# A four-layer graph network on one core: the second linear layer on halves of the array's rows, and edge updates that gather target rows as three bf16 products

## The chip, the cores and the metric

The kernel runs on one core of a Trainium2 chip. The metric is the device time of one execution, in microseconds (us). The core has five engines with a queue each: PE (TensorE) with a side queue PEld for its weight loads, DVE (VectorE), ACT (ScalarE), POOL (GpSimd) and SP (SyncE, which here only issues DMAs). Each engine takes its own instructions in order.

## The reference, cut to what matters

12500 nodes of 16 features, 412500 directed edges (400000 and one loop per node) with 8 features each. Four graph layers run one after the other, each after a layer norm and a relu:

```python
h = relu(layernorm(x)); x = x + L0(h)   # tensor-product message, summed at row ends
h = relu(layernorm(x)); x = x + L1(h)   # message by an edge's own 16x16 matrix
h = relu(layernorm(x)); x = x + L2(h)   # encoder, then two rounds of the block below
h = relu(layernorm(x)); x = x + L3(h)   # two graph convolutions
```

Layer L2 is the one the change is about. With 64 features per node and edge:

```python
def _mlp(x, w0, b0, w1, b1):
    return silu(x @ w0 + b0) @ w1 + b1
n = _ln(_mlp(node_feat, ...)); e = _ln(_mlp(edge_feat, ...))     # encoder
for s in range(2):
    ce = concatenate([e, n[senders], n[receivers]], axis=-1)
    e = e + _ln(_mlp(ce, edge_blk_w0[s], edge_blk_b0[s], edge_blk_w1[s], edge_blk_b1[s]), ...)
    agg = segment_sum(e, receivers, num_segments=num_nodes)
    n = n + _ln(_mlp(concatenate([n, agg]), node_blk_w0[s], ...), ...)
```

So every edge has its feature vector multiplied by a first matrix, the sender's and receiver's rows added (they are multiplied per node beforehand), a silu, a second 64x64 matrix (the "second linear layer"), a layer norm, and a sum at its receiver.

## The kernel before, in words

**Nodes and slots.** Nodes are padded to 12544 and lie in 98 windows of 128 targets. A sort puts every edge into a slot of its target's window: per window 32 blocks of 128 regular slots, ordered by the sender's cell, and 5 blocks of overflow slots (TC, TO; TT is 37).

**Prologue.** Weights and biases are loaded to on-chip tiles by DMAs on SP's queue (`load_w`, `load_b`, `pair_diag`, `bias_rows`, L103 to L289), the sum arrays in DRAM are set to zero from a memory tile of zeros (L322 to L327), then X is loaded, normed (`relu_ln`, L1600) and multiplied to a first message table (`table128`, L1602).

**Sort.** `sort_edges` (L366 on) first finds where each window's edges start (`window_starts`, which loads all targets as `ws_di` and counts on DVE). Then a loop over 98 windows and 5 more steps (LAG) has an order written out by hand: `look_up`, `rank` on DVE, `scatter` on POOL (35 indirect DMAs of a window's records to `cells`, L597), and the layer-L0 products of the window five steps back.

**Pair stages.** The encoder (`Encoded`) and the edge updates 0 and 1 (`Updated`, `l2_cells(s)`) run over 49 pairs of windows in `over_pairs` (L1300). A pair has 10 chunks: c = 0 to 7 with 4 regular blocks, c = 8 with 4 overflow blocks, c = 9 with 1. The order of PE, DVE, ACT and SP is written by hand: slot c of the loop carries work of the new pair (first layer and silu of chunk c, second layer of chunk c−1) and of the old pair (normalizing and summing at targets). Per slot, in this order: `load_features` (SP), `hot_rows(c+1)`, `hidden(c)`, for the old pair `normed` (at c = 0), `scale(c)` and `features(c-1)`, then `output(c-1)`, `activate(c)`, `to_targets(c-1)`, and DVE's reduction. A pair starts with `start()` and `hot_rows(0)`; it ends with `total` (tile got2, on ACT).

**One chunk of an edge update on PE**, in the code's names:

- L1507: the edge features by w0e, on four 64x64 quadrants of the array, for two chunks at once.
- L1514, two forms, called by the helper `half`: first the target rows `td` (64 columns) by the one-hot tile `hot_dt`, 128x256 at a time (L1520), then the table of sender rows by the one-hot tile `hot_st` (32 small products, "hs" below). Two column halves of the array are used in turn.
- L1254: transposes of the old pair's y (edge update 0 and encoder).
- L1216 and L1218 (`outs`): bias as a product of ones, then for each block one product with a 128x128 block-diagonal weight: two slots' 64 features share the 128 rows.
- L1273 (`to_targets`): sums at targets by one-hot rows hot2, 16 instructions.

**The other engines in a chunk.** DVE makes `hot_dt` and `hot_st` (L1490, L1491, L1494 for overflow: is_equal of byte places and the partition's number), reduces squares (L1224), scales y (L1233) and makes hot2 (L1238). ACT does silu (L1209), squares and copies the second layer's result out of PSUM (L1221, L1223), and lod, got2 once a pair. POOL fetches overflow senders' rows (L1467, indirect DMAs).

**PSUM.** The 8 banks in these stages are pt=2, po=5, pa=1; hidden and outs take from po.

**Node tables.** Before an edge update, `tables_l2` (L1648) multiplies the nodes to a table of 128 columns; `take` puts half of it in `t_src` and half, with the bias, in `t_dst` (f32). An update loads `td` from `t_dst`; for s = 1, DVE adds a row `be_w0e` to it at the start of each pair (L1479).

An older form in this kernel makes one-hot rows on ACT: a byte minus a column number, absolute (L630, L1059), then relu(1 − x) (L631, L1060).

Of the kernel before, what the change touches and what calls it, by code (L numbers as in the profile page):

```python
# [19 lines left out]
P = 128  # L20
# [27 lines left out]
def tile_gnn(ctx: ExitStack, tc: tile.TileContext, a: dict, out: bass.AP):  # L48
# [23 lines left out]
    usual = dict(pt=2, po=5, pa=1)  # L72
    summing = dict(pt=2, po=4, pa=2)

    def bank(tag):
        pool, bufs = now[0]
        return pool.tile([P, 512], F32, name=tag, bufs=bufs[tag])
# [53 lines left out]
    def pair_diag(name, src, centered):  # L131

        d = consts.tile([P, P], F32, name=name)
        two = consts.tile([P, 64], F32, name=name + "_2")
        v.memset(d, 0.0)
        sp.dma_start(two[0:64, :], src)
        sp.dma_start(two[64:128, :], src)
        if centered:
            center(two, 64)
        v.tensor_copy(d[0:64, 0:64], two[0:64, :])  # L140
        v.tensor_copy(d[64:128, 64:128], two[64:128, :])
        return d

    def bias_rows(name, src, centered):

        b = consts.tile([3, 64], F32, name=name + "_f")
        sp.dma_start(b, row_bc(src, 64, 3))
        if centered:
            center(b, 64)
        part = consts.tile([3, 3, 64], BF16, name=name + "_p")  # L150
# [10 lines left out]
        r = consts.tile([P, 8, 64], BF16, name=name)  # L161
        v.memset(r, 0.0)
        v.tensor_copy(r[0:3], acc[:, None, :].to_broadcast([3, 8, 64]))
        return r.rearrange("p t f -> p (t f)")
# [27 lines left out]
    wml = load_w("wml", a["L0_gnn_W_msg_lin"], 16, 16)  # L192
    v.tensor_scalar(wml, wml, 0.25, None, op0=ALU.mult)
    wupd = load_w("wupd", a["L0_gnn_W_upd_tp"].rearrange("i h k -> i (h k)"), 16, 256)
    v.tensor_scalar(wupd, wupd, 1.0 / 16.0, None, op0=ALU.mult)
    wul = load_w("wul", a["L0_gnn_W_upd_lin"], 16, 16)
    v.tensor_scalar(wul, wul, 0.25, None, op0=ALU.mult)
    w1t = load_w("w1t", a["L1_w_iao"], 16, 128)
    w1c = consts.tile([P, 16], F32, name="w1c")
    for j in range(8):  # L200
        sp.dma_start(w1c[16 * j:16 * j + 16, :], a["L1_w_iao"][:, 16 * j:16 * j + 16])
    b1_l1 = load_b("b1_l1", a["L1_gnn_bias"], 16)

    p2 = "L2_gnn_"
    ne_w0 = load_w("ne_w0", a[p2 + "node_enc_w0"], 16, 64)
    ne_b0 = load_b("ne_b0", a[p2 + "node_enc_b0"], 64)
    ne_w1 = load_w("ne_w1", a[p2 + "node_enc_w1"], 64, 64)
    center(ne_w1, 64)
    ne_b1 = load_b("ne_b1", a[p2 + "node_enc_b1"], 64)
    center(ne_b1, 64)  # L210
    ne_g = load_b("ne_g", a[p2 + "node_enc_g"], 64)
    ne_be = load_b("ne_be", a[p2 + "node_enc_beta"], 64)

    ee_w0 = consts.tile([P, 8, 64], F32, name="ee_w0")
    v.memset(ee_w0, 0.0)
    for t in range(TS):
        sp.dma_start(ee_w0[8 * t:8 * t + 8, t % 8, :], a[p2 + "edge_enc_w0"])
    ee_w0 = ee_w0.rearrange("p t f -> p (t f)")

    ec_w0 = consts.tile([P, 8, 64], F32, name="ec_w0")  # L220
    v.memset(ec_w0, 0.0)
    for t in range(8):
        sp.dma_start(ec_w0[WORDS * t:WORDS * t + 8, t, :], a[p2 + "edge_enc_w0"])
        sp.dma_start(ec_w0[WORDS * t + W_ONE:WORDS * t + W_ONE + 1, t, :], row_bc(a[p2 + "edge_enc_b0"], 64, 1))
    ec_w0 = ec_w0.rearrange("p t f -> p (t f)")
    ee_b0 = bias_rows("ee_b0", a[p2 + "edge_enc_b0"], False)
    ee_w1 = pair_diag("ee_w1", a[p2 + "edge_enc_w1"], True)
    ee_b1 = bias_rows("ee_b1", a[p2 + "edge_enc_b1"], True)
    ee_g = load_b("ee_g", a[p2 + "edge_enc_g"], 64)
    ee_be = load_b("ee_be", a[p2 + "edge_enc_beta"], 64)  # L230
# [8 lines left out]
    ee_g2 = twice("ee_g2", a[p2 + "edge_enc_g"])  # L239
    ee_be2 = twice("ee_be2", a[p2 + "edge_enc_beta"])  # L240

    eb, nb = [], []
    for s in range(2):
        w0, f = a[p2 + "edge_blk_w0"][s], {}
        f["w0e"] = pair_diag(f"eb_w0e{s}", w0[0:64, :], False)
        f["w0sd"] = consts.tile([64, 128], F32, name=f"eb_w0sd{s}")
        sp.dma_start(f["w0sd"][:, 0:64], w0[64:128, :])
        sp.dma_start(f["w0sd"][:, 64:128], w0[128:192, :])
        f["b0"] = load_b(f"eb_b0{s}", a[p2 + "edge_blk_b0"][s], 64)
        f["w1"] = pair_diag(f"eb_w1{s}", a[p2 + "edge_blk_w1"][s], True)  # L250
        f["w1x"] = consts.tile([P, P], F32, name=f"eb_w1x{s}")
        v.memset(f["w1x"], 0.0)
        sp.dma_start(f["w1x"][0:64, 64:128], f["w1"][64:128, 64:128])
        sp.dma_start(f["w1x"][64:128, 0:64], f["w1"][0:64, 0:64])
        f["b1"] = bias_rows(f"eb_b1{s}", a[p2 + "edge_blk_b1"][s], True)
        f["g"] = load_b(f"eb_g{s}", a[p2 + "edge_blk_g"][s], 64)
        f["be"] = load_b(f"eb_be{s}", a[p2 + "edge_blk_beta"][s], 64)
        f["g2"] = twice(f"eb_g2{s}", a[p2 + "edge_blk_g"][s])
        eb.append(f)
        f = {}  # L260
        f["w0"] = load_w(f"nb_w0{s}", a[p2 + "node_blk_w0"][s], 128, 64)
        f["b0"] = load_b(f"nb_b0{s}", a[p2 + "node_blk_b0"][s], 64)
        f["w1"] = load_w(f"nb_w1{s}", a[p2 + "node_blk_w1"][s], 64, 64)
        center(f["w1"], 64)
        f["b1"] = load_b(f"nb_b1{s}", a[p2 + "node_blk_b1"][s], 64)
        center(f["b1"], 64)
        f["g"] = load_b(f"nb_g{s}", a[p2 + "node_blk_g"][s], 64)
        f["be"] = load_b(f"nb_be{s}", a[p2 + "node_blk_beta"][s], 64)
        nb.append(f)

    eb[0]["sum_be"], eb[1]["sum_be"] = consts.tile([P, 64], F32, name="sum_be"), eb[1]["be"]
    v.tensor_add(eb[0]["sum_be"], eb[0]["be"], ee_be)

    be0 = twice("eb_be2", a[p2 + "edge_blk_beta"][0])
    be_w0e = consts.tile([P, 64], F32, name="be_w0e")
    with banks(**usual):
        pb0 = bank("pa")
        pe.matmul(pb0[:, 0:64], lhsT=be0[0:64, :].to_broadcast([64, P]), rhs=eb[1]["w0e"][0:64, 0:64], start=True,
                  stop=True)
        v.tensor_copy(be_w0e, pb0[:, 0:64])  # L280
    dec_w0 = load_w("dec_w0", a[p2 + "dec_w0"], 64, 64)
    dec_b0 = load_b("dec_b0", a[p2 + "dec_b0"], 64)
    dec_w1 = load_w("dec_w1", a[p2 + "dec_w1"], 64, 16)
    dec_b1 = load_b("dec_b1", a[p2 + "dec_b1"], 16)
    gw1 = load_w("gw1", a["L3_w1_t"], 16, 32)
    gb1 = load_b("gb1", a["L3_gnn_b1"], 32)
    gw2 = load_w("gw2", a["L3_w2_t"], 32, 16)
    gb2 = load_b("gb2", a["L3_gnn_b2"], 16)
# [34 lines left out]
    with tc.tile_pool(name="prep", bufs=1) as wk:  # L323
        zero = wk.tile([P, (C + 1) * 64], F32, name="zero")
        v.memset(zero, 0.0)
        for t in [*g_l0, g_l1, *g_l2, *g_gc, t_acc]:
            sp.dma_start(t.rearrange("(p c) d -> p (c d)", p=P), zero[:, :t.shape[0] // P * t.shape[1]])  # L327
# [1477 lines left out]
```

## Time and profile before

| | |
|---|---|
| Median of 11 runs | 19122.32 us (19106.53 to 19156.79) |
| The profiled execution's own time | 19120.87 us |
| Its span | 19119.1 us |
| PE, PEld, DVE, ACT, POOL busy | 12907.0, 10331.6, 12477.1, 6089.7, 7062.4 us |
| Mean granted TensorE clock | 0.791 |

| Stage | Span, us | Length | Share |
|---|---|---|---|
| Prologue | 0 to 178 | 178 | 0.9% |
| Sort and L0 products | 178 to 7240 | 7062 | 36.9% |
| Encoder and L0's rest | 7240 to 9380 | 2140 | 11.2% |
| L1 with its node work | 9380 to 10813 | 1433 | 7.5% |
| Node work, tables for update 0 | 10813 to 10986 | 173 | 0.9% |
| Edge update 0 | 10986 to 13922 | 2936 | 15.4% |
| Node work, tables for update 1 | 13922 to 14137 | 215 | 1.1% |
| Edge update 1 | 14137 to 16550 | 2413 | 12.6% |
| Rest: node work and L3 | 16550 to 19119 | 2569 | 13.4% |

How to read it. Stage bounds were read from the trace by where a stage's lines begin and end. The middle period of a pair, from one pair's lod copy (L1200) to the next, is 43.0 us in the encoder, 59.8 in edge update 0 and 48.8 in edge update 1. A group line has the line in the code, engine, operation, tile names (out<-in), shape, count, then busy time in us and mean ns of one, then the engine's idle time just before them and what ended it. PE instructions overlap, so the mean duration of one is longer than the time from one start to the next; for PE it is the start-to-start time that adds up. The granted clock is TensorE's, as a share of full speed.

### The profile page before, as it was taken

How to read it: one execution, taken by the hardware profiler on the slowest of the kernel's cores; microseconds unless marked ns; L12 is line 12 of the kernel's file. 1: busy time of each engine (PE TensorE's matmuls, PEld its weight loads, DVE VectorE, ACT ScalarE, POOL GpSimd, SP SyncE). 2: the span in 40 equal slices, each digit the busy share in tenths (PEclk: the TensorE clock that was granted, in tenths of full speed). 3: DMA queues.
4: the chain of work that ended last, by engine and by line, in shares of the span. 5: the costliest groups of instructions: out<-in, count | busy, mean ns of one | idle time of the engine just before them, and what ended most of it. 6: DMA issues, size and time to landing. Idle time of an engine off the chain costs nothing. (4 is left out here: it accounts for less than half of the span.)

```text
span 19119.1 us, 387064 instructions
## 1 busy us (share of the span) xinstructions
PE 12907.0 (68%) x161327; PEld 10331.6 (54%) x161327; DVE 12477.1 (65%) x23622; ACT 6089.7 (32%) x10025; POOL 7062.4 (37%) x6387
## 2 busy tenths in 40 slices
PE   1444444444444448999788688888879999756566
PEld 1443434444443447777577666666656666644444
DVE  5555555555555556777788777777757777655555
ACT  0111111111111125555377522222223333334343
POOL 3444444444444443444344311111113322144344
PEclk6666666666666669999899899999989999966666
DMA  1101100001000004444366544444434333266666
GB/s 67 28 25 28 28 28 25 28 28 28 25 28 28 25 24 105 126 125 126 107 169 172 145 130 136 136 136 135 135 109 118 116 114 115 75 172 176 160 175 169
DMA packets 1361577, 1827.92 MB, mean 96 GB/s; under 512 B 501594, under 2 KB 794970, under 8 KB 1358526
## 3 DMA queue, kind: packets, MB, share of 16 engines
q1 hardware_dynamic: 1079624, 1721.34, 29.6%
q0 software_dynamic: 258720, 76.68, 4.1%
q8 instruction: 1275, 20.89, 0.5%
q10 hardware_dynamic: 21462, 4.95, 0.1%
q14 instruction: 496, 4.06, 0.1%
HBM read 1296.64 MB, written 504.92 MB: 94 GB/s over the span
## 5 line engine op out<-in xcount | busy, mean ns | idle before, releaser
L597 POOL DMA_INDIRECT cells<-rec,s_row x3430 | 3295.5, 961 | 3632.0 <-DVE s_row L593 2527.5
L1467 POOL DMA_INDIRECT xo<-t_src,c x980 | 1246.3, 1272 | 4424.2 <-DMA c<-cells 2207.2
L641 PE MATMUL pl<-win,hot_dt 128*128 128x128 f32 x7252 | 1445.8, 372 | 2110.9 <-DVE wide L650 1736.5
L641 PEld LDWEIGHTS pl<-win,hot_dt 128*128 128x128 f32 x7252 | 1342.5, 281 | 2177.1 <-DVE wide L650 1774.0
L650 DVE TENSOR_TENSOR wide<-pl,c 128x512 f32<-128x512 f32 x980 | 602.9, 645 | 2726.2 <-remote 2519.8
L675 PE MATMUL acc<-parted,hot_s 128*98 128x64 f32 x6272 | 1186.1, 344 | 1676.6 <-issue 1663.9
L675 PEld LDWEIGHTS acc<-parted,hot_s 128*98 128x98 f32 x6272 | 1101.4, 266 | 1781.8 <-issue 1765.3
L1221 ACT ACTIVATE sq<-po 128x512 f32<-128x512 f32 (+1 forms) x1470 | 832.3, 566 | 3694.1 <-PE po L1218 2853.3
L1273 PE MATMUL pa<-hot,y 128*64 128x128 f32 x21756 | 1674.8, 284 | 240.2 <-issue 155.0
L1224 DVE TENSOR_REDUCE nsum<-sq 128x8 f32<-128x512 f32 (+1 forms) x1470 | 947.1, 644 | 1141.7 <-ACT sq L1221 1099.9
L1011 POOL DMA_INDIRECT xo<-t_gc,c x980 | 1032.4, 1054 | 1586.2 <-DMA c<-cells 556.8
L1238 DVE TENSOR_TENSOR hot<-iota_row,lod 128x512 f32<-128x512 f32 x2352 | 1517.3, 687 | 0.0
L1273 PEld LDWEIGHTS pa<-hot,y 128*64 128x64 f32 x21756 | 1211.9, 138 | 529.1 <-issue 334.8
L812 POOL DMA_INDIRECT g_l<-summed,row x490 | 857.7, 1750 | 1411.9 <-ACT summed L808 1075.9
L1082 DVE TENSOR_REDUCE x<-po 128x128 f32<-128x384 f32 x1176 | 650.9, 553 | 1048.1 <-remote 470.4
L666 ACT ACTIVATE parted<-pre 32x256 f32<-32x256 f32 x784 | 325.1, 415 | 3157.8 <-issue 2913.3
L1514 PE MATMUL po<-hot_dt,td 128*64 128x256 f32 (+2 forms) x7056 | 1012.7, 404 | 9.9 <-DVE hot_dt L1490 8.5
L631 ACT ACTIVATE hot_dt<-off,one_col 128x2048 f32<-128x2048 bf16 (+1 forms) x294 | 473.9, 1612 | 1652.6 <-remote 1631.1
L1059 ACT ACTIVATE off<-places,minus_col 98x1024 bf16<-98x1024 uint8 x784 | 898.9, 1147 | 269.5 <-DMA places<-slot_lo 224.5
L1209 ACT ACTIVATE hidn<-po 128x512 f32<-128x512 f32 (+1 forms) x1470 | 855.9, 582 | 329.1 <-PE po L1514 269.4
L1233 DVE TENSOR_TENSOR y<-y,nr 128x512 f32<-128x512 f32 (+1 forms) x1470 | 949.2, 646 | 5.1
L1091 DVE TENSOR_TENSOR hot_d<-iota_row,c 128x1024 f32<-128x1024 f32 (+1 forms) x882 | 949.6, 1077 | 0.0
(380 smaller groups left out, 27677.7 us busy)
## 6 DMA issues: line engine op xcount, KB each, us to landing
hot_dk<-keep_t SPq DMA_DIRECT2D x588, 512.0 KB
e_feat<-ft SPq DMA_DIRECT2D x882, 256.0 KB
ft<-e_feat SPq DMA_DIRECT2D x882, 256.0 KB
c<-cells SPq DMA_DIRECT2D x392, 296.0 KB
keep_t<-hot SPq DMA_DIRECT2D x392, 256.0 KB
ud<-slot_lo SPq DMA_DIRECT2D x98, 1024.0 KB
c<-cells SPq DMA_DIRECT2D x147, 592.0 KB
us<-slot_lo SPq DMA_DIRECT2D x98, 784.0 KB
```

The costliest lines, as they stand in the source:

```text
L597: ins = gp.indirect_dma_start(out=self.cells, out_offset=bass.IndirectOffsetOnAxis(ap=self.row[:, t:t + 1], axis=0), in_=self.rec[:, t, :] ...
L641: pe.matmul(pl[:, t * P:(t + 1) * P], lhsT=self.hots[t0 // 16][:, o:o + P], rhs=self.win, start=True, stop=True, skip_group_check=True)
L675: pe.matmul(acc[t // 8][0:C, o:o + 64], lhsT=self.hot[:, t, :], rhs=self.k["parted"][self.g % 2][:, t, :, :].rearrange("p q f -> p (q f)") ...
L1011: gp.indirect_dma_start(out=out[:, t, :], out_offset=None, in_=table, in_offset=bass.IndirectOffsetOnAxis(ap=c[:, TC + t, W_SRC:W_SRC + 1] ...
L1059: sc.activation(off, u, AF.Abs, bias=minus_col[:C, :])
L1091: v.tensor_tensor(o[:, :k, :], bc_mid(iota_row, k), bc_last(self.c[:, t0:t0 + k, W_LD], P), ALU.is_equal)
L1224: return lambda: v.tensor_reduce(self.sums[:, 8 * c:8 * c + 2 * k], sq[:, :2 * k, :], AX.X, ALU.add)
L1233: v.tensor_tensor(w, w, bc_last(self.r[:, 8 * c:8 * c + 2 * k], 64), ALU.mult)
L1238: v.tensor_tensor(hot[:, w].rearrange("p (h t) d -> p h t d", h=2), iota_row[:, None, None, :].to_broadcast([P, 2, 2, P]), lo[:, :, :, Non ...
L1273: pe.matmul(self.acc[64 * w:64 * w + 64, 0:P], lhsT=lhsT, rhs=rhs, start=c == 0 and i < 2, stop=c == 9 and i >= len(work) - 2, skip_group_ ...
L1467: gp.indirect_dma_start(out=self.xo[:, w, t, :], out_offset=None, in_=t_src[s], in_offset=bass.IndirectOffsetOnAxis(ap=self.c[:, w, TC + t ...
L1514: pe.matmul(out[o:o + 64], lhsT=lhsT, rhs=rhs, start=start, stop=stop, skip_group_check=True)
```

## The change

Four edits come together.

1. **Second layer.** `outs` works on row halves: for each block two products, rows 0 to 63 and rows 64 to 127 of the array, each with a 64x64 weight, into the two banks of a new tile `pw` (one buffer of two banks; po goes from 5 to 3). The bias is two products of up to 256 columns. ACT's square and copy read both banks by one access pattern. The tile y goes from 12 to 11 buffers.
2. **Target rows.** `td` is loaded from a new DRAM table `t_dst3` of three bf16 parts, whose sum is exactly the f32 row; `hot_dt` is bf16, and each product becomes three.
3. **One-hot rows by ACT.** `hot_dt` is made by ACT (Abs, then Relu, with a one-buffer tile `off`) in place of DVE, and `hot_rows` runs two chunks ahead in place of one (3 buffers); `activate(c)` comes before `output(c-1)`.
4. **Prologue.** The weights' loads, their centering and the zeroing of DRAM sums become steps of a generator `weights`, one of which is taken at the start of each step of the sort's loop; `window_starts` runs first, and X is loaded after the targets.

`tables_l2` writes the three parts: ACT copies to bf16, POOL subtracts; for s = 1 it adds `be_w0e` there.

```diff
-    usual = dict(pt=2, po=5, pa=1)
+    usual = dict(pt=2, po=3, pa=1, pw=1)
...
+    def weights(zero):
...
+        for name, src, centered in pairs:
+            d = consts.tile([P, P], F32, name=name)
+            two = consts.tile([P, 64], F32, name=name + "_2")
+            v.memset(d, 0.0)
+            sp.dma_start(two[0:64, :], src)
+            sp.dma_start(two[64:128, :], src)
+            diags[name] = (d, two, centered)
+            yield
...
+        n = zero.shape[1]
+        for t in [*g_l0, g_l1, *g_l2, *g_gc, t_acc]:
+            w = t.shape[0] // P * t.shape[1]
+            for o in range(0, w, n):
+                k = min(n, w - o)
+                sp.dma_start(t.rearrange("(p c) d -> p (c d)", p=P)[:, o:o + k], zero[:, :k])
+                yield
...
+                zero = one.tile([P, C * 17], F32, name="zero")
+                v.memset(zero, 0.0)
+                others = weights(zero)
                 for g in range(ND + LAG):
+                    if g:
+                        next(others, None)
...
-            k, po, hid = self.blocks(c), bank("po"), self.hid
-            n = k * P
-            pe.matmul(po[:, :n], lhsT=ones_r, rhs=b1[:, :n], start=True, stop=False, skip_group_check=True)
+            k, pw, hid = self.blocks(c), bank("pw"), self.hid[c]
+            for half in range(2):
+                pe.matmul(pw[:, half, :k * 64], lhsT=ones_r, rhs=b1[:, :k * 64], start=True, stop=False,
+                          skip_group_check=True)
             for j in range(k):
-                pe.matmul(po[:, j * P:(j + 1) * P], lhsT=hid[:, j * P:(j + 1) * P], rhs=w1, start=False,
-                          stop=j == k - 1, skip_group_check=True)
+                for h in range(2):
+                    x, half = slice(64 * h, 64 * h + 64), h ^ swapped
+                    pe.matmul(pw[:, half, j * 64:(j + 1) * 64], lhsT=hid[x, j * P:(j + 1) * P],
+                              rhs=w1[x, 64 * half:64 * half + 64], start=False, stop=j == k - 1, skip_group_check=True)
+            out = pw[:, :, :k * 64].rearrange("p h (j f) -> p j h f", f=64)
             sq = self.ed.tile([P, 8, 64], F32, name="sq")
-            sc.activation(flat(sq)[:, :n], po[:, :n], AF.Square)
-            self.ys[c] = self.ed.tile([P, 4, P], F32, name="y", bufs=12)
-            sc.copy(flat(self.ys[c])[:, :n], po[:, :n])
+            sc.activation(sq[:, :2 * k, :].rearrange("p (j h) f -> p j h f", h=2), out, AF.Square)
+            self.ys[c] = self.ed.tile([P, 4, P], F32, name="y", bufs=11)
+            sc.copy(self.ys[c][:, :k, :].rearrange("p j (h f) -> p j h f", h=2), out)
...
                     new.hot_rows(0)
+                    new.hot_rows(1)
...
-                    if new and c < 9:
-                        new.hot_rows(c + 1)
+                    if new and c < 8:
+                        new.hot_rows(c + 2)
...
+                    if new and c < 10:
+                        new.activate(c)
                     if new and c:
                         reduce = new.output(c - 1)
-                    if new and c < 10:
-                        new.activate(c)
...
-                    v.tensor_scalar(hd, of(self.ud), iota_col, None, op0=ALU.is_equal)
+                    u, o, d = of(self.ud), off, hd
                     v.tensor_scalar(hs, of(self.us), iota_col[:C, :], None, op0=ALU.is_equal)
...
+                sc.activation(o, u, AF.Abs, bias=minus_col)
+                sc.activation(d, o, AF.Relu, bias=one_col, scale=-1.0)
...
-                        for h in range(2):
-                            half(h, po[:, 2 * w * P:2 * (w + 1) * P], self.td[:, w, :], hd[:, w, h, :])
+                        for part in parts:
+                            for h in range(2):
+                                half(h, po[:, 2 * w * P:2 * (w + 1) * P], self.td[:, w, part], hd[:, w, h, :])
...
+    with tc.tile_pool(name="ws", bufs=1) as wk:
+        window_starts(wk)
...
+            for j in range(3):
+                sc.copy(parts[:, :k, j, :], was[:, :k, :])
+                if j < 2:
+                    gp.tensor_tensor(rest[:, :k, :], was[:, :k, :], parts[:, :k, j, :], ALU.subtract)
+                was = rest
+            sp.dma_start(rows(t_dst3[s])[:, c:c + k, :], parts[:, :k].rearrange("p k j f -> p k (j f)"))
```

## The prediction

> **What bounds the kernel now.** I read the sums by stage first, because the engine shares of the whole run mix eight stages. Columns: length, busy time of PE, PEld, DVE, ACT and POOL with instruction counts, granted TensorE clock, DMA share, GB/s.
>
> ```profile
> 0.00:178.00 178.00, 27.83 (x69) 12.97 (x70) 92.93 (x209) 3.19 (x5) 5.64 (x16) 0.88 0.36 134
> 178.00:7240.00 7062.00, 3072.96 (x17248) 2825.20 (x17247) 4005.48 (x6863) 1317.70 (x1585) 3295.64 (x3431) 0.62 0.10 27
> 7240.00:9380.00 2140.00, 1996.60 (x19306) 1558.60 (x19306) 1580.25 (x3479) 1212.41 (x2303) 856.93 (x490) 0.99 0.46 124
> 10986.00:13922.00 2936.00, 2626.47 (x32237) 1928.14 (x32235) 2176.49 (x4109) 756.50 (x1566) 539.52 (x484) 0.93 0.47 134
> 14137.00:16550.00 2413.00, 2265.37 (x30424) 1667.18 (x30421) 1876.65 (x3670) 756.50 (x1567) 692.89 (x484) 0.99 0.39 113
> ```
>
> Row by row: prologue, sort, encoder, edge update 0, edge update 1. The last three are PE's (93, 89 and 94% busy); the sort is not (44%). In the sort one wait rules, by the page:
>
> ```profile
> L597 POOL DMA_INDIRECT cells<-rec,s_row x3430 | 3295.5, 961 | 3632.0 <-DVE s_row L593 2527.5
> ```
>
> POOL waits 2527.5 us for DVE's ranks, about 26 us in each of 98 windows: there DVE work adds directly.
>
> Then one chunk of edge update 0, as the timeline shows it (start, time covered):
>
> ```profile
> 12003.85 0.38 PE L1216 MATMUL po<-eb_b,ones_r 128*128 128x512 bf16 x1
> 12003.85 1.08 PEld L1218 LDWEIGHTS po<-eb_w1x,hidn 128*128 128x128 f32 x8
> 12004.07 1.05 PE L1218 MATMUL po<-eb_w1x,hidn 128*128 128x128 f32 x8
> 12005.05 0.85 PEld L1273 LDWEIGHTS pa<-hot,y 128*64 128x64 f32 x16
> ...
> 12010.59 0.21 PEld L1507 LDWEIGHTS po<-ft,eb_w0e 64*64 64x64 f32 x8 [0.17 <-issue]
> ```
>
> From L1218's start to that of L1273's first load is 0.98 us: eight instructions (an f32 matmul is two) at 112 ns, plus 0.09 for the change of tile shape. Is 112 ns the moving side's price or the weight load's? Another line loads the same 128 f32 columns and moves only 16:
>
> ```profile
> L806 PEld LDWEIGHTS po<-over,same x980: 186/192/192, 7295.1 to 9370.9; 128*128 128x128 f32 x196
> L806 PE MATMUL po<-over,same x980: 262/263/283, 7295.1 to 9370.9; 128*128 128x16 f32 x196
> ```
>
> Its starts are also 112 ns apart and its durations nearly L1218's (280 and 193 ns), so the load sets the pace. Last, the groups of edge update 1 that the change touches or that show its start-of-pair wait:
>
> ```profile
> L1273 PE MATMUL pa<-hot,y 128*64 128x128 f32 x7252 | 561.7, 281 | 102.9 <-DVE hot L1238 73.1 <-issue 22.6 <-DVE hot L1243 0.2
> L1514 PE MATMUL po<-hot_dt,td 128*64 128x256 f32 (+1 forms) x3528 | 491.1, 395 | 8.2 <-DVE hot_dt L1490 8.2
> L1490 DVE TENSOR_SCALAR hot_dt<-ud,iota_col 128x1024 f32<-128x1024 uint8 x390 | 293.3, 752 | 2.6 <-PE po L1514 2.6
> L1209 ACT ACTIVATE hidn<-po 128x512 f32<-128x512 f32 x490 | 285.3, 582 | 139.7 <-PE po L1514 139.7
> L1218 PE MATMUL po<-eb_w,hidn 128*128 128x128 f32 x1960 | 275.2, 280 | 2.2 <-ACT hidn L1209 0.8 <-issue 0.2
> ```
>
> PE's largest wait is 73.1 us, 1.5 per pair of windows: to_targets(0) waits for DVE's first hot2, queued behind rsqrt. In edge update 0 that wait is about 2.07 per pair, seen as one run of L1514's 32 taking 3.1 us instead of 1.03 before the transposes at 12053.
>
> **The change part by part.** The sum is made against the profiled execution: span 19119.1, own time 19120.9 (1.8 around the span), 1.4 under the median 19122.3.
>
> *Second layer on halves (1470 chunks: 3 stages x 49 pairs x 10).* Eight instructions of 128 rows, 128 moving columns become sixteen of 64 rows, 64 moving columns, on two row halves. Each still loads 128 columns. L1507's eight loads (132 ns each, four quadrants, both row halves) lie in 0.21 us, so loads of different tiles run together; eight pairs at 112 ns are then what eight instructions are now. Added: one more change of shape, since the bias stays at full height (0.09 as at L1218 to L1273), an exposed first load (0.107, a 128-column load) less a shorter last product (0.054, the 64 columns): **+0.149 us per chunk**. Bounds: below, −0.28, if loads hide and the 58 ns per pair of L1514's hs rows (64 columns loaded and moved) holds: 8 x (58 − 112) + 149. Above, +1.05, if the halves' loads queue: 8 x 112 more. I take the value by L1507, the only row with both row halves loading at once.
>
> A rule speaks here. The Trainium skill, TensorEngine Tiling (Array Packing), Theoretical Speedup, gives up to 2x for a contraction of 64; by it the eight pairs would halve and the sum fall by some 630 us, as in rival one. The same page under Key Properties says changing the tiling mode drains the array, which speaks against the change, and this trace's 0.09 is that cost. TensorE: Matmul & The Clock Gate, LDWEIGHTS, says load time follows the columns and not the rows, as the 16-column row above suggests; by it the sum stays mine.
>
> *td as three bf16 parts.* Four pairs of 256 moving f32 columns at 215 ns become six. The bf16 price is not in this trace at this shape; a bf16 pass is one of the two f32 passes, so 109 ns (the cadence of L1273's 128 f32 columns, the same number of passes of columns). 864 − 654 = **−0.21 per chunk**, −1.95 per pair with the short last chunk; bounds −0.46 (58 per pair) and +0.43 (215 still). Beside it 13 more PE instructions per chunk; where PE waits for "issue" that may cost, and I put it at nothing because issue is 0.5% of edge update 1.
>
> *hot_dt by ACT.* DVE loses 0.75 us per chunk, ACT gains Abs and Relu: 1.15 each (L1059 and L1060, 98x1024, 1147 and 1150 ns). ACT's chunk goes from 1.7 to 4.0 us against PE's 4.5 to 5.1: it fits in steady running. Not at the start of a pair, where ACT's queue holds got (0.37), lod (0.31), Abs(0), Relu(0), Abs(1), Relu(1), Abs(2), Relu(2), then silu(0). PE ends the old pair's to_targets(9), does L1507 (1.02) and needs Relu(0): 0.1 + 0.37 + 0.31 + 2.3 + 0.1 − 1.02 = 2.2 idle, against 0.25 now, +1.95. Then silu(0) stands behind four more one-hot operations (4.6), and outs(0) behind it: PE has td(0), hs, td(1), hs, about 3.4, and waits some +0.57 after handoffs. The DVE wait at to_targets(0) (2.07, 1.5) goes: DVE's queue has 0.85 less ahead of rsqrt and PE arrives 2 later. Per pair, with td −1.95 and outs +1.49: edge update 0, −0.46 + 1.95 + 0.57 − 2.07 = 0.0; edge update 1, −0.46 + 1.95 + 0.57 − 1.5 = +0.56, taken +0.1 and +0.6. Encoder: outs alone, 1.49 x 0.93 busy = +1.4. 49 x 2.1 = **+103**. Bounds: one-hot operations at 1.0 give +20; at 1.3 +190; at 2.0 (L630's 2048 columns, twice the size) ACT's chunk would be 5.7, over PE's, about +700.
>
> *Clock.* The granted clock comes in windows of about 3.4 us: every window with PE under 0.4 busy is followed by half clock, about half of those between 0.45 and 0.6. Edge update 1 stays at 0.99 with worst windows at 0.56. A 2.2 us wait in one window leaves 0.35; alignment puts it there in about half of 98 pairs, and a half-clock window costs some 2.4: **+115** (0 to +330). The Trainium skill's clock gate section in TensorE: Matmul & The Clock Gate likewise ties idle windows to a half clock; the rows above are enough without it.
>
> *Node tables.* Each take (49 in all) adds three ACT copies of 128x256 (0.38 each, between L704's 0.27 at 128 columns and 0.587 at 512), two POOL subtractions and a DMA, in one chain with hand-offs: 2.5 us against the 1.22 that DVE takes now. 49 x 1.3 = **+65** (+20 if POOL and ACT overlap across takes; +110 if POOL needs 0.5 each). The DVE add leaving the pair start is 0.28 of cover only.
>
> *Prologue into the sort loop.* The weights' DMAs hold SP's queue to 56 us, the zeroing to 92; X lands at 92.7, and dst only at 143.7. With both gone, dst lands about 10, then window starts 29, layer norm 15, table 28, sort constants 6: 88 of 178, −90. Into the loop go 77 steps: about 100 small DVE instructions (0.14 as L128's, to 0.25 with gaps) and memsets, 27 us, on DVE's ranks that POOL waits for; the zeroing DMAs run where DMA is 10% busy. A late matmul +1. **−62** (−95 if DVE's steps fall beside POOL's transfers; 0 if each zeroing transfer also delays a window by 3.6).
>
> Sum: 19120.9 − 62 + 65 + 103 + 115 = 19343, about **19345**, +1.2%.
>
> **Rivals.** *One, faster: the row halves aren't bound by loads.* Then outs costs −0.28, not +0.149, per chunk: 19345 − 0.43 x 1470 = 18715. For it: loads of other tiles overlap matmuls in L1507. Against it: L806's rows. It decides wherever outs' cadence falls under 97 ns per pair, where the whole sum reaches 19120. *Two: the halves' loads queue.* 8 x 112 ns x 1470 = +1317, to 20660. For it: all loads come from one PE queue; against it: L1507. *Three: ACT's chain at the pair start is short or hidden, and tables overlap.* No clock loss (−115), pairs +20 (−83), tables +20 (−45): 19100, about what it is now; for it, ACT is 26 to 31% busy; against it, its in-order queue. *Four, within the first: the clock falls at every pair,* +215 more, 19560.
>
> **How the numbers follow.** 0.2%, 38 us, is about what a measurement of this kernel can tell from no change. Forecast (19180 to 19620, its own range) 0.57; rival one 0.20; rival two 0.11; rival three 0.12, of which 0.05 is faster, 0.06 the same and 0.01 slower. So faster 0.25, same 0.06, slower 0.69. The range runs from rival one's time to just over the forecast's own, 18715 to 19700; rival two and the tails stay outside.
>
> **What would show it.** Right: outs' pairs 112 ns apart with about 1.13 us from its first start to to_targets'; td's group 0.65; PE at a pair's start waiting about 2 us for ACT's hot_dt; ACT near 75% busy in both updates; clock under 0.95 in edge update 1; prologue about 90, sort about 27 longer. Wrong: outs' pairs near 58 or 224 ns; a one-hot operation far from 1.15; the wait at the start taken by nobody. The sum fails most easily at the cadence of the row halves, which no row shows, and next at the clock.

## The result and the profile after

The changed kernel takes 19561.5 us (median of 8 runs, 19522.7 to 19623.5) against 19126.0 (31 runs): ratio 1.023, interval 1.022 to 1.024, 436 us slower. The forecast had the sign and half the size (+223), inside its range. The profiled execution of the changed kernel has a span of 19573.6 us, 454.5 more than before.

The sums by stage of the changed kernel, in the same columns and order as before (prologue, sort, encoder, edge update 0, edge update 1):

```profile
0.00:82.00 82.00, 25.08 (x63) 11.63 (x63) 63.05 (x90) 3.30 (x5) 3.55 (x14) 0.99 0.29 109
82.00:7138.00 7056.00, 3045.74 (x17254) 2803.78 (x17254) 4032.40 (x6982) 1317.77 (x1586) 3297.47 (x3434) 0.62 0.10 29
7138.00:9306.00 2168.00, 2032.36 (x23422) 1575.12 (x23422) 1579.98 (x3478) 1207.59 (x2303) 867.99 (x487) 1.00 0.46 122
10948.00:14043.00 3095.00, 2694.94 (x38121) 2086.45 (x38121) 1898.74 (x3622) 1791.24 (x2547) 475.43 (x490) 0.89 0.45 128
14274.00:17000.00 2726.00, 2403.06 (x36309) 1870.84 (x36309) 1575.46 (x3133) 1794.10 (x2548) 563.00 (x490) 0.91 0.35 102
```

Both updates grew, update 1 by twelve per cent, and their granted clock fell to 0.89 and 0.91. The 454.5 us by stage, each cut at the first lod copy and the last got2 of its pairs:

| Stretch | Before | After | Difference |
|---|---|---|---|
| Prologue and sort, to the encoder's first pair | 7244.7 | 7137.9 | −107 |
| Encoder | 2131.6 | 2167.6 | +36 |
| L1, node work, tables for update 0 | 1601.0 | 1642.7 | +42 (tables 27) |
| Edge update 0 | 2945.3 | 3095.1 | +150 |
| Node work, tables for update 1 | 204.2 | 230.9 | +27 |
| Edge update 1 | 2421.5 | 2725.2 | +304 |
| Rest | 2570.8 | 2574.2 | +3 |

Where in a pair? One steady chunk of the changed kernel in the timeline:

```profile
15407.74 0.85 PE L1558 MATMUL po<-hot_dt,td 128*64 128x256 bf16 x12
...
15408.42 1.10 PE L1558 MATMUL po<-hot_st,tab 98*64 98x64 f32 x32
...
15409.45 0.39 PE L1255 MATMUL pw<-eb_b,ones_r 128*128 128x256 bf16 x2
...
15409.77 1.11 PE L1260 MATMUL pw<-eb_w1x,hidn 64*128 64x64 f32 x16
```

td's twelve take 0.68 before the hs products start (0.86 to 0.91 before), the bias 0.32 (0.23 before) and the sixteen row-half products 1.04 up to to_targets at 15410.81 (0.98 before). A steady chunk is 0.06 us shorter: not the loss. The waits of PE in update 1, in total, number of times and longest; first of the changed kernel, then of the kernel before:

```profile
PE po L1558 <- ACT hot_dt L1539: 112.8, 87, 1.9
PE po L1558 <- issue: 106.6, 208, 1.1
...
PE pw L1260 <- issue: 30.9, 58, 1.0
...
PE pw L1255 <- issue: 16.6, 26, 1.1
PE pa L1316 <- DVE hot L1281: 6.1, 8, 4.9
```

```profile
PE pa L1273 <- DVE hot L1238: 73.1, 56, 4.9
...
PE pa L1273 <- issue: 22.6, 90, 1.0
...
PE po L1514 <- issue: 5.9, 9, 1.2
```

At the start of a pair a wait for ACT's hot_dt took the place of the one for DVE's hot2, as forecast. New is "issue": PE waits for nothing that the profile shows, in the middle of a group whose data has long been there. Part of one such place:

```profile
15418.33 0.96 POOL L1511 DMA_INDIRECT xo<-t_src,c  x1 [0.30 <-issue]
15418.46 1.03 PEld L1558 LDWEIGHTS po<-hot_st,tab 98*64 98x64 f32 x25
15418.57 1.07 PE L1558 MATMUL po<-hot_st,tab 98*64 98x64 f32 x24
15419.60 0.94 POOL L1511 DMA_INDIRECT xo<-t_src,c  x1 [0.30 <-issue]
15419.99 0.36 PE L1558 MATMUL po<-hot_st,tab 98*64 98x64 f32 x5 [0.36 <-issue]
...
15420.72 0.22 PE L1558 MATMUL po<-hot_st,tab 98*64 98x64 f32 x1 [0.38 <-issue]
15420.85 0.95 POOL L1511 DMA_INDIRECT xo<-t_src,c  x1 [0.31 <-issue]
15421.43 0.19 PEld L1558 LDWEIGHTS po<-hot_st,tab 98*64 98x64 f32 x2 [1.18 <-issue]
15421.44 0.33 PE L1558 MATMUL po<-hot_st,tab 98*64 98x64 f32 x2 [0.50 <-issue]
```

One group of 32 starts at 29 per us for 0.8 us, and then its last eight come a few at a time, 0.7 us apart, while POOL issues one indirect load of xo (rows of overflow senders) after another. I call this the slow stretch. Adding up each group of a pair over its undisturbed length (means over the pairs whose groups come in the same order, us a pair): between the second w0e group and the overflow chunks, update 0 lost 9.0 before and 11.9 after, update 1 lost 2.6 and 8.35. (In plain times from the second w0e group to the first overflow product: 41.46 and 43.68 us in update 0, where the undisturbed runs e6 and e5 below have 32.51 and 31.84; 32.22 and 37.23 in update 1, against 29.63 and 28.95.) So (2.9 + 5.7) x 49 = 420 us of growth in the slow stretch; starts of pairs +1.14 and +1.40, 124 us; the remainder of the two stages is shorter by some 90. All the rest of the program nets to about nothing.

### The profile page after: what moved, and what is told of

Same layout as the page of the kernel before. It is cut to its first block, busy times and chain, and to the rows that moved or that the text cites. A ratio compares the mean times of both kernels' runs of the same rounds, so it can differ in the third digit from the quotient of the medians.

```text
span 19573.6 us, 419284 instructions
## 1 busy us (share of the span) xinstructions
PE 13138.0 (67%) x177203; PEld 10699.4 (55%) x177203; DVE 11904.1 (61%) x22618; ACT 8211.6 (42%) x12135; POOL 6944.0 (35%) x6487
## 5 line engine op out<-in xcount | busy, mean ns | idle before, releaser
L1511 POOL DMA_INDIRECT xo<-t_src,c x980 | 1038.4, 1060 | 4645.7 <-DMA c<-cells 2345.1
L1264 ACT ACTIVATE sq<-pw 128x512 f32<-128x512 f32 (+1 forms) x1470 | 831.1, 565 | 1017.1 <-PE pw L1260 752.0
L1558 PE MATMUL po<-hot_st,tab 98*64 98x64 f32 x25088 | 1042.8, 234 | 149.9 <-issue 145.2
L1558 PE MATMUL po<-hot_dt,td 128*64 128x256 bf16 (+2 forms) x10584 | 886.9, 297 | 307.5 <-ACT hot_dt L1539 229.0
L1558 PEld LDWEIGHTS po<-hot_st,tab 98*64 98x64 f32 x25088 | 979.4, 149 | 193.1 <-issue 188.6
L1539 ACT ACTIVATE hot_dt<-off,one_col 128x1024 bf16<-128x1024 bf16 x980 | 1065.0, 1087 | 31.9
```

Source lines behind the costliest of these rows:

```text
L1264: sc.activation(sq[:, :2 * k, :].rearrange("p (j h) f -> p j h f", h=2), out, AF.Square)
L1511: gp.indirect_dma_start(out=self.xo[:, w, t, :], out_offset=None, in_=t_src[s], in_offset=bass.IndirectOffsetOnAxis(ap=self.c[:, w, TC + t ...
L1539: sc.activation(d, o, AF.Relu, bias=one_col, scale=-1.0)
L1558: pe.matmul(out[o:o + 64], lhsT=lhsT, rhs=rhs, start=start, stop=stop, skip_group_check=True)
```

## The experiments

The first runs were to tell two theories of the stretch apart. S: the bulk transfers for the next pair fill the DMA engines and PE's instructions are late, the more so as PE has more of them (13 more per chunk). R: one-hot rows two chunks ahead free the byte-place tiles us and ud a slot sooner, so these transfers fall on denser chunks.

**Row halves alone (e1)**, on the kernel before: the new `outs` and `pw` only.

```diff
-    usual = dict(pt=2, po=5, pa=1)
+    usual = dict(pt=2, po=3, pa=1, pw=1)
```

> The kernel before with the second layer on row halves alone (nothing else of the change). Both theories: steady chunks 0.15 us longer, +222 over 1470 chunks, since the pairs of row-half products still start 112 ns apart. Theory S (PE runs short of instructions while the next pair's transfers fill the DMA engines, the more so the more instructions a chunk has): the slow stretch near chunk 6 or 7 also grows in both edge updates, 9 of the change's 13 added PE instructions per chunk being here; of its growth of 377 us some 260, so about 19600. Theory R (the stretch grew because one-hot rows two chunks ahead free the byte-place tiles a slot earlier, so the transfers fall on denser chunks): the stretch stays as before, about 19345.

Measured 19402.0 against 19117.9, ratio 1.0137 (1.0115 to 1.0159), +284. The steady price is as both theories had it; the stretch lost 8.9 and 3.7 us a pair against 9.0 and 2.6, +51. Nine more PE instructions per chunk do not make 377.

**bf16 target rows alone (e2)**, on the kernel before:

```diff
-                self.td = td = ed.tile([P, 2, 64], F32, name="td")
...
+                self.td = td = ed.tile([P, 2, 192], BF16, name="td")
...
-                hd = self.hd[c] = ed.tile([P, 2, 2, 2 * P], F32, name="hot_dt")
+                hd = self.hd[c] = ed.tile([P, 2, 2, 2 * P], BF16, name="hot_dt")
```

> The kernel before with target rows as three bf16 parts alone; hot_dt is bf16 and still made by DVE, one chunk ahead. Both: td's group 0.21 shorter per chunk, -190; tables +54; sum -136, so about 18990. Theory S: 4 of the 13 added PE instructions are here, so the stretch grows by about 115 and the sum is near 19100. Theory R: 18990.

Measured 19019.5, ratio 0.9945 (0.9927 to 0.9963), −98: this part alone gains. The middle of a pair lost 6.0 and 2.8 us: the stretch did not grow.

**One chunk ahead (e3)**, on the changed kernel:

```diff
-                    new.hot_rows(1)
...
-                    if new and c < 8:
-                        new.hot_rows(c + 2)
+                    if new and c < 9:
+                        new.hot_rows(c + 1)
```

> The changed kernel with hot_rows one chunk ahead again (ACT still makes hot_dt). Theory R: the byte-place tiles come free a slot later, the slow stretch goes back to its size in the kernel before, -377, so about 19180, with the start of a pair little changed. Theory S: the stretch stays within some 80 us of the changed kernel's; about 19560, or above it where hot_dt is now late.

Measured 19252.1, ratio 1.0065 (1.0046 to 1.0084): 1.65% of the 2.3% are gone, with all 13 extra instructions still there and hot_dt still made by ACT. The stretch lost 9.5 and 2.8 us, nearly as in the kernel before. So far R.

**Without the byte places (e4)**, on the changed kernel:

```diff
...
+                if cls.kept is None:
+                    cls.kept = (self.places(0, 0, TC, "us2", 1), self.places(1, 0, TC, "ud2", 1),
+                                self.places(1, TC, TT, "uo2", 1))
+                self.us, self.ud, self.uo = cls.kept
```

> The changed kernel with the byte places us, ud and uo loaded for the first pair of each update only; all other pairs use the first pair's (this leaves out 96 of 98 loads of three tiles, and the edges gathered are then others). Both theories lay the slow stretch to PE waiting for instructions behind these transfers: without them it should nearly vanish, some -19 us a pair in update 0 and update 1 together (11.6 and 7.9), about -900, near 18650. If it stays, the cause is another (POOL's indirect transfers, the feature loads, the clock).

Measured 19612.2 (one run), no better than the changed kernel. With these loads gone the DMA engines are far less busy where PE is slowest (chunks 6 and 7 of update 1: mean share 0.24 against 0.57), and the stretch is as long (11.95 and 8.6). R's mechanism and S fall together. What is left in the stretch is POOL. Sorting the starts of the hs products of the changed kernel's update 1 by whether POOL ran an xo load in the 1.2 us before: of some 3400 with one, 242 come after a gap of over 0.25 us; of some 8700 without, one. That is theory X: PE is short of instructions while POOL's indirect transfers follow one another without a pause. That it is instructions that PE lacks is the theory's wording and is not shown; the profile shows idle time that it puts down to nothing.

**Without the indirect loads (e5, e6)**, on the changed kernel and on the kernel before:

```diff
...
+                if cls.over is not None:
+                    self.xo = cls.over
+                    return
...
```

> The changed kernel with POOL's indirect loads of overflow senders' rows (xo) made for the first pair of each update only and reused by the others (this leaves out 96 of 98 sets of ten; the rows added in chunks 8 and 9 are then others). Theory X (PE is short of instructions while POOL's indirect transfers follow one another without a pause): the slow stretch, 11.9 us a pair in update 0 and 8.4 in update 1, goes, about -990, near 18570. Theory S (the byte places and other bulk transfers on the DMA engines): the stretch stays, about 19560.

> The same left out of the kernel before. Theory X: its stretch of 9.0 and 2.6 us a pair goes, about -567, near 18555; then what is left between the two kernels is starts, steady chunks, tables and prologue, within 100 us of each other. Theory S: no change, 19120.

Measured 18774.9 and 18757.6 (one run each; the kernel before beside them 19362.2, on another chip than e1 to e4; the changed kernel with its loads was not run on this one). The two updates by sums, e5 first:

```profile
11073.00:13603.00 2530.00, 2413.62 (x38121) 1957.48 (x38121) 1897.44 (x3623) 1790.34 (x2548) 9.56 (x10) 0.97 0.48 151
13844.00:16169.00 2325.00, 2178.15 (x36308) 1732.63 (x36308) 1569.86 (x3133) 1787.85 (x2547) 9.61 (x10) 0.97 0.36 113
```

```profile
11103.00:13635.00 2532.00, 2405.12 (x31999) 1880.74 (x32241) 2185.32 (x4113) 756.42 (x1567) 10.62 (x10) 0.98 0.48 150
13839.00:16140.00 2301.00, 2173.73 (x30280) 1648.81 (x30428) 1872.51 (x3672) 755.97 (x1567) 10.52 (x10) 0.99 0.35 113
```

POOL has 10 instructions where it had 490; update 0 lasts 2530 and 2532, update 1 2325 and 2301, and the clock is back at 0.97 to 0.99. The stretch is gone from both (0.0 to 0.2 us a pair), and with it nearly all of the difference: 17 us between the two kernels. So the indirect loads make the stretch, and the lower clock came with it: in chunks 6 and 7 of the changed kernel the granted clock is 0.73 and 0.80 in the two updates, and 1.00 in e5. How much of the stretch is the clock's part was not separated.

**The same loads, spread out (e7)**, on the changed kernel, two per slot in slots 5 to 9, each behind an index copy in DVE's queue:

```diff
+                    if then and 5 <= c < 10:
+                        then.fetch(2 * (c - 5))
...
+                at = self.ed.tile([P, 1], I32, name="at", bufs=2)
+                v.tensor_copy(at, self.c[:, w, TC + t, W_SRC:W_SRC + 1].bitcast(I32))
+                gp.indirect_dma_start(out=self.xo[:, w, t, :], out_offset=None, in_=t_src[s],
+                                      in_offset=bass.IndirectOffsetOnAxis(ap=at, axis=0))
```

> The changed kernel, all work kept, with the ten indirect loads of a pair spread over slots 5 to 9, two per slot some 2.5 us apart, by an index copy on DVE ahead of each. Theory X with the spacing deciding: most of the growth of 377 goes, 19100 to 19300. If the number of indirect loads alone counts and not their spacing, it stays near 19560, or moves by less than 100.

Measured 19057.9 against 19362.2, ratio 0.9853 (0.9831 to 0.9874): from 2.3% slower than the kernel before to 1.5% faster, beyond what was expected. The loss in the middle is 0.1 us a pair in each update. With all ten loads kept the stretch is gone: their spacing decides, not their number. (The spread loads also begin two slots sooner and read a copied index; these were not tried apart.) Some came back at the end of a pair (10.0 and 8.1 us against 7.2 and 6.3), where DVE waits for the two index tiles (412 us in update 0) and for the cells.

**Prologue and target rows with spread loads (e8)**, no row halves, hot_dt on DVE:

> The kernel before with the prologue moved into the sort, target rows as three bf16 parts with hot_dt on DVE one chunk ahead, and the same spread of indirect loads; no row halves, no ACT one-hot rows. Prologue -107 (stage times of the changed kernel), target rows -98 (measured), and by theory X up to -400 of the stretch: between 18500 and 18800. Without an effect of the spread: 18915.

Measured 19212.2, ratio 0.9923 (0.9905 to 0.9941): less than expected: 150 us under the kernel before, where 205 were expected without any effect of the spread. The stretch is gone here too (0.2 and 0.6), but the end of a pair takes 12.8 and 9.7 us: with hot_dt in DVE's queue the waiting index copies hold up more.

**Ten index tiles, slots 6 to 10 (e9, e10), and two more variants (e11, e12).** e12 is e9 without the row halves. f3, f2 and f4 are the kernels of e9, e11 and e12 again, on another chip, and f1 is the changed kernel. For these eight the same kernel before took 15559 and 15566 us, one of the chips having the number of the one in e1 to e4. What differed can be read from the sort, from the row of DVE's first step after PE's products; first the kernel before in the condition of the result, then the changed kernel in this one (f1):

```profile
L650 DVE TENSOR_TENSOR wide<-pl,c 128x512 f32<-128x512 f32 x980 | 602.9, 645 | 2726.2 <-remote 2519.8 <-PE pl L641 153.6 <-issue 52.6
```

```profile
L689 DVE TENSOR_TENSOR wide<-pl,c 128x512 f32<-128x512 f32 x980 | 599.0, 644 | 221.5 <-PE pl L680 220.9 <-issue 0.6
```

The 2519.8 us of waiting, 26 us in each window, are gone: PE works on while POOL runs its 35 indirect transfers (each still 0.96 us), and windows follow every 45 us in place of 71. "remote" stands for a release that the profile can trace to no instruction of this core. In the condition of the result it is not DVE's alone; the sort of the kernel before:

```profile
DVE wide L650 <- remote: 2519.8, 114, 28.8
...
PE acc L675 <- issue: 1663.9, 1396, 3.2
ACT hot_dt L631 <- remote: 1631.1, 92, 18.6
```

Where DVE's L650 waited, the PE products that it reads had ended a median of 20.6 us before it began; in f1 it begins as they end. In the two edge updates the "remote" waits of ACT and DVE come to 506 us before, 982 in the changed kernel and 749 in e3, and to none in e5, e6, e7 and f1. So under POOL's transfers not only PE's next instruction is late, but also the releases that others wait for; what is held back inside PE, or on the way from it, no view here shows. In the condition of f1 POOL's transfers do not slow PE, and the slow stretch is missing from every kernel, spread or not (0.0 to 0.9 us a pair). Ratios below are to the kernel before in the same condition, and these runs say nothing on the stretch itself. What changes the condition is not known.

> The changed kernel with the indirect loads spread over slots 6 to 10 and ten buffers for the index copies, so that DVE no longer waits for an index tile to come free (412 us of waits in update 0 with two buffers) nor for the cells (136). Theory X: the slow stretch stays away and the 2.8 and 1.8 us that the first spread added at the end of a pair go: another 150 to 220 below it, ratio to the kernel before 0.975 to 0.98. If the waits of DVE were covered: 0.985 as before.

> The changed kernel with the indirect loads spread over slots 6 to 10 (ten index tiles). Where PE is slowed: the stretch of 11.9 and 8.4 us a pair goes nearly whole, 0.975 to 0.98 of the kernel before. Where not: 1.005 as measured.

> The changed kernel, beside the others on one chip. Where PE is slowed by POOL's indirect transfers (the kernel before near 19120 to 19360): ratio 1.02. Where it is not (the kernel before near 15560): the stretch is absent in both, prologue -107, encoder +36, tables +54, starts +134, steady -44, so about +70 and a ratio of 1.005.

e9 1.0053 (1.0035 to 1.0071), f3 1.0031 (1.0016 to 1.0045), f1 1.0041 (1.0027 to 1.0055). The changed kernel, which was 2.3% slower, is 0.4% slower where PE isn't slowed; and spreading the loads, which gained 1.5% on the kernel before in e7, is worth nothing there (f3 is 22 us under f1). This fits the finding from the other side. What ten index tiles would do in the condition of the result was not measured.

> The changed kernel with hot_dt made by DVE again (bf16, still two chunks ahead). The start of a pair loses ACT's chain, some 2 us a pair, but the wait for DVE's first hot2 comes back, 1.5 to 2. Theory X with DVE's part (DVE's hot2, y and hot_st hold POOL's indirect loads back, which leaves PE pauses to catch up): more DVE work lengthens the run of ten indirect loads from 11.3 and 13.2 us back towards 13 and 16, and the stretch shrinks by most of 377: ratio to before 1.003 to 1.01. If ACT's or PE's own load sets the stretch: 1.02.

```diff
+                    v.tensor_scalar(hd, of(self.ud), iota_col, None, op0=ALU.is_equal)
...
-                sc.activation(o, u, AF.Abs, bias=minus_col)
-                sc.activation(d, o, AF.Relu, bias=one_col, scale=-1.0)
```

> The changed kernel with hot_dt made by DVE again (bf16, two chunks ahead). Where PE is slowed: if denser indirect loads made the stretch grow, DVE's work holds them back again, the run of ten takes about 13 and 16 us, and the stretch shrinks by most of 377, ratio near 1.005; if PE's instruction count did, it stays and the ratio is 1.015 to 1.025. Where PE is not slowed: 1.019 as measured.

1.0190 and 1.0172: taking the one-hot rows back from ACT costs 210 us (f2 against f1). The start of a pair is 13.0 and 11.4 us against 10.7 and 10.8. Whether DVE's work sets the stretch could not be asked in this condition. Its part in the spacing can be read: the ten loads of a pair take 12.2 and 14.7 us from the first start to the last in both, against 11.5 and 13.5 in f1, a small part of the way back to the 13.2 and 16.3 of the kernel before.

> As e9 but with the second layer whole (128 rows). Steady chunks 0.15 us shorter, 1470 x 0.15 = -220 against e9, so a ratio 0.0115 below e9's. If the halves' cost is covered in part by other waits, less: -100 to -200.

> As f3 with the second layer whole. Where PE is slowed: 0.96 to 0.97 of the kernel before, faster than both kernels. Where not: 0.989 as measured.

> Prologue move and bf16 target rows, hot_dt on DVE one chunk ahead, whole second layer, the same better spread. Steady chunks 0.21 shorter than before and no slow stretch: update 0 near 51.1 - 1.95 = 49.2 a pair and update 1 near 46.5 - 1.95 = 44.6 against 59.7 and 49.0 before, -107 prologue, +54 tables: -780, ratio 0.96. If DVE (index copies in its queue, hot_dt still on it) now sets the end of a pair: 0.975 to 0.985.

e12 0.9891 (0.9868 to 0.9915), f4 0.9887 (0.987 to 0.9903), e10 0.9918 (0.9888 to 0.9948), whose gain is a fifth of what it was to be, as the stretch that made most of it was not there to be gained. f4 is 219 us under f3: the row halves' price, expected at 220. The change without the halves and with spread loads beats both kernels in this condition by 1.1 and 1.5%; e7 and e2 do so in that of the result by 1.5 and 0.55% of the kernel before.

## Why the prediction was wrong

**The step that failed** is a sentence under the target rows: "Beside it 13 more PE instructions per chunk; where PE waits for 'issue' that may cost, and I put it at nothing because issue is 0.5% of edge update 1". Measured: 420 us. It failed three times. The reading was too low: PE's "issue" waits in update 1 add up to 40 us, 1.7% of it. I looked at update 1 alone, where the stretch was 2.6 us a pair; update 0 lost 9.0 us a pair in it, 15% of its period, and I had no term for it. Update 0's largest "issue" wait in the kernel before:

```profile
PE pa L1273 <- issue: 132.4, 202, 1.4
```

And I tied it to the number of instructions, where e1 and e3 show that the number hardly matters (+51 us for nine of thirteen; some 35 for all thirteen at one chunk ahead). What matters is that POOL's ten indirect loads run closely packed, which no step spoke of.

Why did they pack? POOL's row in update 1, in the kernel before, the changed kernel and e3:

```profile
L1467 POOL DMA_INDIRECT xo<-t_src,c x484 | 694.6, 1435 | 1639.6 <-PE po L1514 1150.9 <-DMA c<-cells 230.5 <-issue 132.9
```

```profile
L1511 POOL DMA_INDIRECT xo<-t_src,c x490 | 563.0, 1149 | 2099.3 <-DMA c<-cells 1117.3 <-PE po L1551 531.8 <-PE pa L1316 207.6
```

```profile
L1510 POOL DMA_INDIRECT xo<-t_src,c x490 | 666.6, 1361 | 1733.3 <-PE pa L1316 821.3 <-DMA c<-cells 377.5 <-PE po L1550 268.7
```

A load takes 1435 ns on average before, 1149 after, 1361 in e3; the middle one of both updates takes 0.95 us in all three, but 177, 54 and 188 of 980 take over 1.8 us. From the first start to the last of a pair's ten (medians, updates 0 and 1), beside the loss in the stretch, us a pair:

| Run | Ten loads | Loss |
|---|---|---|
| Kernel before | 13.2, 16.3 | 9.0, 2.6 |
| e1, row halves alone | 13.0, 17.0 | 8.9, 3.7 |
| e2, bf16 target rows alone | 13.2, 15.9 | 6.0, 2.8 |
| e3, one chunk ahead | 13.0, 15.5 | 9.5, 2.8 |
| Changed kernel | 11.5, 13.4 | 11.9, 8.35 |
| e4, no byte places | 11.5, 13.3 | 11.95, 8.6 |
| e7, spread | 23.9, 23.5 | 0.1, 0.1 |

The loss goes with the packing, save for e2's update 0, which loses another 2 us behind the first overflow product. The long loads have one thing in common: all 177, 54 and 188 overlap DVE's hot2, an f32 comparison of two tiles in on-chip memory (376, 251 and 271 loads do, so an overlap alone is not enough), while of the 96 loads of the kernel before that had hot_dt running 0.3 to 0.6 us after their start none was long. The Trainium skill, SBUF — State Buffer, section SBUF: two separate sides, tells why a load can be held: POOL writes the descriptors of its own DMAs, and certain DVE operations lock it out of a port that they share. It names operations with two inputs in on-chip memory among them, against a POOL operation that reads that memory; the overlaps agree, and no run here shows the port itself.

By this reading the stalled loads gave PE its pauses, and the changed kernel took most of them away. It did not do so by taking hot_dt off DVE: e3 has hot_dt on ACT too, and there the loads are held and the stretch is nearly that of the kernel before. What e3 puts back is one chunk ahead in place of two. That the loads' spacing decides is shown (e7), that two chunks ahead brings the close packing about is shown (e3); that it does so by shifting DVE's hot2 against the loads is argued from the overlaps and was not tried.

**Right, or nearly:**

- Row halves: +0.149 us per chunk forecast; measured 0.150 (0.984 + 0.226 to 1.038 + 0.322), and −219 for taking them back (f4 against f3). L1507's parallel loads and L806's 16-column row were the right rows: a 128-column f32 load sets 112 ns, with 16, 64 or 128 columns moving behind it. Rivals one and two fall. The 97 ns per pair given as the first one's turning point should have been 93: 225 us over 1470 x 8 pairs.
- td: −0.21 forecast, −0.21 to −0.23 measured.
- The wait at a pair's start: 2.2 us idle forecast, 1.99 measured (w0e to td 3.005 us against 1.019), then 0.7 at the first hs products and 0.3 and 0.6 at the first bias. Net of the DVE wait that went: +1.14 and +1.40 with what the clock lost there, 124 us; the terms for both updates' starts and the clock came to 35 + 115 = 150, or 195 without the steady chunks' −45 that the first of them holds.
- The clock: forecast to fall at pair starts; it fell mostly in the stretch. At the starts it is 0.93 and 0.92, low in a quarter to a third of the pairs and not in half; in chunks 6 and 7 it is 0.73 and 0.80. Right in size for update 1's granted clock (0.91, under 0.95), for another reason. Rival four, the clock falling at every pair, has 19560, next to the 19561.5 measured: luck, by the same numbers.
- ACT: near 75% busy forecast in both updates, 58 and 66% measured, since the stretch made them longer; 71 and 77% in e5, without it.
- Encoder: +36 against +68. The row halves' price was right: +71 in e1 alone, and 72 between f4 and f1. What had no term is the new order of steps, which takes some 35 back: the encoder lasts 2202.9 us in e1, 2186.8 in e3, where the silu comes before the second layer, and 2167.9 in the changed kernel, which is also two chunks ahead.
- Node tables: +54 against +65.
- Prologue: −107 against −62. The first scatter starts 90 us sooner as forecast (−90), but the sort itself did not take the 27 us of small DVE steps: it is 17 us shorter. They were put on DVE's path to POOL, from POOL's wait for DVE; but DVE itself waits 2519.8 us there (the "remote" row above), and that left room for them.

Without the stretch the sum of what was measured is 454 − 420 = +34, a fifth of a per cent; f1 measured 0.41% where there is no stretch. So the sign, too, came mostly from a cause that the forecast did not have, and was luck to that extent: its +115 for the clock and its 77 too much at the encoder and the prologue stood in the place of the stretch.

## What to carry to other kernels

Look for places where an engine waits for "issue" inside a group whose data is all there, and ask which other engine is busy just then; a stage's share of issue time hides a burst that returns every period. A change in when one engine does its work can hurt an engine that shares nothing with it in the code: one-hot rows made two chunks ahead in place of one let POOL's indirect transfers close up, and these held PE up. Where a queue of indirect transfers isn't urgent, pace it: here it was worth 1.5% over the kernel before in one condition and nothing in the other.

## What was not expected of the hardware

- While POOL runs indirect transfers 1.25 us apart, PE starts a few matmuls every 0.7 us (five, one and two in the lines above) in place of 29 per us; gaps of over 0.25 us in the hs group followed an indirect load in 242 of 243 cases in the changed kernel's update 1.
- Releases are late as well: in the sort DVE went on a median of 20.6 us after the PE products that it needed had ended.
- The same kernel before takes 19120 to 19360 us where this happens and 15560 where it does not; in the sort alone it is 26 us of each window's 71. What switches it is open.
- Two row halves load their 128 columns at once, one pair every 112 ns, as one full-height load does.
